# A graph layer with an edge index built beside its matrix products: pauses for the index, two conversions swapped in its round, and a split first load

## The chip, the cores and the metric

The kernel runs on one core of one Trainium2 chip. The metric is the device time of one execution in microseconds; a time with "median" is the median of several executions. The profile is of one execution, and its times count from the first instruction of the span.

## The reference

There are 1250 nodes with 1024 features, and 20000 edges, each with a source, a target and one of eight types. Cut to what matters, the reference computes:

```python
h = maximum(layernorm(x), 0)
u = h @ root + bias
for r in range(8):
    mask = (edge_type == r)
    sums = segment_sum(h[src] * mask[:, None], dst, 1250)
    cnt = segment_sum(mask, dst, 1250)
    u = u + (sums / maximum(cnt, 1)[:, None]) @ weight[r]
z = concatenate([u, h], 1) @ w_gate + b_gate
out = x + tanh(u) * z + h * (1 - z)
```

All tensors are float32. Since a mean times a matrix is the mean of the products, the kernel multiplies h by each weight first and gathers rows of the products.

## The kernel before, in words

**Products.** There are eleven 1024x1024 matrices: the eight weights, the root and the two halves of the gate. `step(s, i)` multiplies matrix `s` with a pair of 128-row blocks, `i` from 0 to 4, so a matrix takes five steps. A step is a 2x2 block scheme of Strassen's kind (`product`): up to seven groups of matmuls with 512 columns, each group shown in the trace as eight matmul records. From matrix 1 on, the steps with `i` below 4 leave out one group and put a second, smaller scheme in its place; its pieces of 256 columns (`Second`, L211, four records each) are `fill`s between the groups. After most groups ScalarE (ACT) copies the PSUM bank to an SBUF row: L313, L317, L321, L305 and L341 stand for the first, second, third, S3 and last group. The groups S4 and A12 are added by VectorE (DVE) instead, L298 and L331.

**Calls.** After each group, and after some fills, `product` calls `between(j)`. This makes 7 calls in a step and 35 in a matrix. `between` is `beside` in `step`. It issues the work of the next matrix: in the last step (`i` = 4) the differences of weight blocks `make_t1` (j=1), `make_t2` (j=4) and `make_t3` (j=5), in the first step of the next matrix `make_t4` (j=0) and, for matrices 1 to 3, one difference (`right`) in each of the calls 0 to 3 of the same step. All of these run on DVE (L166, L170, L174, L178, L201). After that `beside` calls `on(j)`.

**The index.** `on(j)` runs one more piece of the generator `index()`, up to its next `yield`. The index has 126 pieces: 18 of layer norm and columns, 86 of `slots`, and 22 of `order`. It begins in matrix 0. `slots` finds for every edge its place in the table of its target node. It takes 40 chunks of 512 edges; each round of its loop has two `yield`s, so it takes two calls:

- a call whose work is mostly ACT's (called the ACT call here): `as_bf16` (L796), four `one_hots` activations (L743) and their Relu (L745), `as_int` (L781, L783), `to_los` (L802, L803); also `load_keys`, which lets SP's queue load `k_bc` and `l_bc` (L774);
- the next call (called the PE call here): `count`, four small matmuls of TensorE (PE) on L761 and DVE additions on L766; `split` on DVE (L789); `place`, four small matmuls on L812, then DVE work (L817 to L836) and the scatters of GpSimd (POOL) on L840.

`place` reads what `to_los` and `as_bf16` made (`to_lo` and `s_b`), and `as_bf16` reads what `split` made. The PSUM tile `ps_n` of `count` has one buffer: the next `count` waits until L766 has read the last one.

`order` sorts nodes by number of edges (L894 on DVE) and lets POOL write and read the sorted tables (L506, L469). After matrix 3, `weights(0)` (L493 on DVE) reads those tables and the gathers of product rows begin (L1014 on POOL, L1022 on DVE).

**The order.** The order of instructions on each engine is the order in which the program issues them (`manual_schedule`); nothing is moved by a planner.

**The start.** `load_x` loads the first two blocks of x (`x0`) by SP's queue, one as two halves and one whole; then come the four blocks of the first matrix and more of x. The layer norm of both (`both`), their transposes (L257) and the copies (L259) stand ahead of the first product.

Of the kernel before, what the change touches and what calls it, by code (L numbers as in the profile page):

```python
# [19 lines left out]
def tile_rgcn_highway(  # L20
# [31 lines left out]
    nc = tc.nc  # L52
# [3 lines left out]
    P = 128  # L56
# [8 lines left out]
    NP = ND // 2  # L65
# [23 lines left out]
    def nrows(d):  # L89
        return min(P, N - d * P)  # L90
# [4 lines left out]
    def nedges(c):  # L95
        return P if c < NCH - 1 else EL
# [349 lines left out]
    steps = iter([(s, i) for s in range(NM - 1) for i in range(NP)])  # L446
# [78 lines left out]
    with ExitStack() as early:  # L525
# [6 lines left out]
        def load_x(i, part, t=None, pieces=1):  # L532
            d = i + part * NP
            n = nrows(d)
            if t is None:
                t = xpool.tile([P, D], F32, name="xt")
            for j in range(pieces):
                at = slice(j * D // pieces, (j + 1) * D // pieces)
                nc.sync.dma_start(t[:n, at], x[d * P:d * P + n, at])
            return t  # L540

        def scratch(i, part):
# [65 lines left out]


        warm = xpool.tile([P, 1], F32, name="warm")  # L610
        nc.scalar.activation(warm, eps, AF.Sqrt)
        x0 = [load_x(0, part, pieces=2 - part) for part in range(2)]
        fac[0].load_first()
        fac[0].load_next()
        fac[0].load_b22()
        x1 = [load_x(1, 0, scratch(NP - 2, 0))]
        fac[0].load_b21()
        x1.append(load_x(1, 1, scratch(NP - 2, 1)))
        x2 = [load_x(2, 0, h_op[2][:, S1:S2 + 1].rearrange("p a k f -> p (a k f)")), load_x(2, 1)]

# [7 lines left out]
        for name, of, pad in (("dst", dst, G * KEYS), ("typ", etype, R), ("src", src, 0)):  # L628
            t = ix0.tile([P, 2, P], I32, name=f"e_{name}")
# [97 lines left out]
        def slots(ix):  # L727
# [118 lines left out]
                    tc.add_to_no_dep_group("scatter", ins.ins)  # L846

            for j in range(ng + 3):
                for f, of in ((one_hots, j), (load_keys, j - 1), (as_int, j - 2), (to_los, j - 2),
                              (None, None), (count, j - 1), (split, j - 2), (place, j - 3),  # L850
                              (None, None), (as_bf16, j - 2)):
                    if f is None:
                        yield
                    elif 0 <= of < ng:
                        f(of)
# [115 lines left out]
        def index():  # L971
            for _ in zip_longest(norms(), columns()):
                yield
            with tc.tile_pool(name="ix", bufs=2) as ix:
                yield from slots(ix)
            yield from order()

        todo = index()
        going = [True]

        def on(j):
            if going[0]:
                going[0] = next(todo, 0) is None

        while going[0]:
            step(*next(steps), on)


    with ExitStack() as edges_part:
# [44 lines left out]
        def edges(g, blocks, to, late=0):  # L1034

            of = u_dram[g - 1] if g else None
            nb = len(blocks)  # L1040
            starts = [late + sum(K[g][d] for d in blocks[:b]) for b in range(nb + 1)]
            leaves = [starts[b + 1] - 1 + GOT for b in range(nb)]
            reads = [max(-1, starts[b] - 5, leaves[b - UB] if b >= UB else -1) for b in range(nb)]
            u, then = {}, {}
            for t in range(-1, leaves[-1] + 4):
                for b, d in enumerate(blocks):
                    if starts[b] <= t < starts[b + 1]:
                        k = t - starts[b]
                        add_slot(u[d], g, d, k, idx[:, g], w_of[:, g], first=g == 0 and k == 0)
                for b, d in enumerate(blocks):  # L1050
                    if t == leaves[b]:
                        then[t + 3] = to(d, u[d])
                if then.get(t):
                    then[t]()
                for b, d in enumerate(blocks):
                    if t == reads[b]:
                        u[d] = new_u(d, of, g)
                yield

        def u_back(g):  # L1060
            def to(d, u):
                n = nrows(d)
                to_rows(u_dram[g][:, :], u[:n], node[:n, g, d:d + 1], f"u{g}")

            return to
# [42 lines left out]
        def beside(e, total, s, i, last):  # L1108


            between = spread(e, total, 7 * ((last - s) * NP + NP - i))
            while s <= last:
                step(s, i, between)
                s, i = next(steps, (NM, 0))
            return s, i

        s, i = next(steps)
        while s <= R0[1]:
            step(s, i)
            s, i = next(steps)  # L1120
# [8 lines left out]
        def with_others(e):  # L1129

            others = other_groups()
            for k, _ in enumerate(e):
                yield
                if k % 2:
                    next(others, None)
            for _ in others:
                pass

        weights(0)
        s, i = beside(with_others(edges(0, range(ND), u_back(0))), sum(K[0]) + 2, s, i,  # L1140
                      R0[2] - 1)
# [6 lines left out]
        for g in range(1, G - 1):  # L1148
# [3 lines left out]
            s, i = beside(e, sum(K[g]) + LATE + 1, s, i, R0[g + 2] - 1)  # L1152
# [4 lines left out]
        with tc.If(passes > 0):  # L1157
# [30 lines left out]
            with tc.For_i(0, passes, 1):  # L1188
# [9 lines left out]
                for c in range(NCH):  # L1198
                    n = nedges(c)
# [92 lines left out]
        while s < NM - 1:  # L1292
# [8 lines left out]
            s, i = next(steps, (NM, 0))  # L1301

        for i in range(NP):
            t = [rows.tile([P, D], F32, name="row") for _ in range(2)]
# [59 lines left out]
```

## Time and profile before

| what | value |
|---|---|
| median of 3 executions | 1375.87 us (1373.83 to 1377.13) |
| the profiled execution: its own time | 1372.16 us |
| the profiled execution: span of the trace | 1370.3 us |
| mean granted TensorE clock | 0.997 |
| PE busy | 1349.8 us |
| DVE busy | 930.5 us |
| POOL busy | 638.7 us |
| ACT busy | 366.7 us |
| one later matrix, without the index (652.32 to 771.08 us) | 118.76 us |

The profiled execution's own time is its span and 1.9 us around it. It is 3.7 us shorter than the median of the three timed executions. A busy time counts the engine's own records; a wait is shown as the idle time ahead of an instruction, with the instruction that ended it. In the first 400 us the index lies beside the products, and ACT and DVE are busier than in the rest of the span.

### The profile page before, as it was taken

Reading aid. Unit: us, or ns where it says so; the run is one execution under the profiler, and the core shown is the slowest. Engines: PE = TensorE matmul, PEld = TensorE weight load, DVE = VectorE, ACT = ScalarE, POOL = GpSimd, SP = SyncE. Lnnn points to the kernel's source line nnn. Section 1 sums busy time; section 2 is a strip of 40 time slices with the busy share of each in tenths; the row PEclk is TensorE's granted clock in tenths of the full one; section 3 lists DMA queues with packets and bytes.
Section 4 is the critical chain, followed back from the end, with each engine's and each line's share of the span. In section 5 each row is a group of like instructions: output and inputs, shape, how many; then the busy total and the mean of one; then the engine's idle time right before and its main releaser. Section 6 shows DMA issues by size and latency. Waiting matters only on the chain.

```text
span 1370.3 us, 12737 instructions
## 1 busy us (share of the span) xinstructions
PE 1349.8 (99%) x3786; PEld 657.9 (48%) x3786; DVE 930.5 (68%) x1842; ACT 366.7 (27%) x793; POOL 638.7 (47%) x567
## 2 busy tenths in 40 slices
PE   7999999999999999999999999999999999999998
PEld 4444455445545544544554454455445445544443
DVE  6956987797678817556665746765564485567985
ACT  3336566566531111111111111111111111121220
POOL 0003655565561633647774334465443253436641
PEclk9999999999999999999999999999999999999999
DMA  8764665956553274379879627787955664586861
GB/s 306 286 204 103 125 139 142 182 108 130 141 132 104 65 216 121 115 235 252 233 268 323 210 103 269 278 291 253 356 202 207 225 243 142 189 293 222 288 204 58
DMA packets 110010, 272.77 MB, mean 199 GB/s; under 512 B 25906, under 2 KB 27936, under 8 KB 109808
## 3 DMA queue, kind: packets, MB, share of 16 engines
q0 software_dynamic: 48864, 128.60, 29.6%
q1 hardware_dynamic: 45232, 111.86, 27.0%
q10 hardware_dynamic: 15840, 31.46, 7.6%
q8 instruction: 30, 0.49, 0.1%
q14 instruction: 44, 0.36, 0.1%
HBM read 214.20 MB, written 80.65 MB: 215 GB/s over the span
## 4 chain that ended last, share of the span: by engine, by line
PE 79%; DVE 6%; issue 6%; DMA 2%; POOL 2%; ACT 1%; POOLq 0%; SPq 0%; DVEq 0%; ACTq 0%
PE ps L284 70%; PE ps L211 8%; DMA l_bc<-los_dram 1%; POOL got L469 1%; DVE seen L766 1%; DVE junk L826 1%; DMA got<-hr_dram,node 0%; DMA h_op<-z_dram,node 0%; PE ps_n L761 0%; POOL out_dram L475 0%; DVE row L1312 0%; DMA got<-y,idx 0%; DVE h_op L1258 0%; DVE u L1225 0%; DVE w L178 0%
## 5 line engine op out<-in xcount | busy, mean ns | idle before, releaser
L284 PE MATMUL ps<-w,h_op 128*128 128x512 f32 x2800 | 1226.8, 594 | 2.0 <-ACT row L321 2.0
L284 PEld LDWEIGHTS ps<-w,h_op 128*128 128x128 f32 x2800 | 527.6, 190 | 616.8 <-issue 600.6
L1014 POOL DMA_INDIRECT got<-y,idx x202 | 259.8, 1286 | 283.4 <-DVE u L1022 187.5
L1022 DVE SCALAR_TENSOR_TENSOR u<-got,w_of,u 128x1024 f32<-128x1024 f32 (+1 forms) x192 | 245.9, 1283 | 124.5 <-DMA got<-y,idx 122.3
L840 POOL DMA_INDIRECT table<-row_col,at_i x157 | 174.8, 1113 | 150.1 <-DVE at_i L836 75.2
L306 DVE TENSOR_TENSOR row<-row,part 128x512 f32<-128x512 f32 x55 | 38.0, 690 | 118.8 <-ACT part L305 118.8
L341 ACT COPY row<-ps 128x512 f32<-128x512 f32 x50 | 29.3, 586 | 236.2 <-PE ps L284 236.2
L298 DVE TENSOR_TENSOR row<-row,ps 128x512 f32<-128x512 f32 x55 | 37.7, 685 | 63.6 <-PE ps L284 56.2
L305 ACT COPY part<-ps 128x512 f32<-128x512 f32 x55 | 32.2, 586 | 177.3 <-PE ps L284 177.3
L313 ACT COPY row<-ps 128x512 f32<-128x512 f32 x55 | 32.2, 585 | 165.8 <-PE ps L284 159.2
L211 PE MATMUL ps<-w,w 128*128 128x256 f32 x288 | 71.3, 380 | 0.0
L321 ACT COPY row<-ps 128x512 f32<-128x512 f32 x55 | 32.2, 585 | 138.4 <-PE ps L284 138.4
L317 ACT COPY row<-ps 128x512 f32<-128x512 f32 x55 | 32.2, 585 | 135.5 <-PE ps L284 128.5
L211 PEld LDWEIGHTS ps<-w,w 128*128 128x128 f32 x288 | 54.4, 190 | 20.9 <-issue 15.3
L766 DVE TENSOR_TENSOR seen<-seen,ps_n 128x110 f32<-128x110 f32 x157 | 42.2, 269 | 27.6 <-PE ps_n L761 23.5
L826 DVE SCALAR_TENSOR_TENSOR junk<-k_bc,key_col,before 128x128 f32<-128x128 int32 x157 | 55.0, 350 | 4.2
L211 PE MATMUL ps<-w,h_op 128*128 128x256 f32 x216 | 55.9, 381 | 0.0
L506 POOL DMA_INDIRECT node_dram<-ids,pos_i x30 | 37.5, 1251 | 39.2 <-issue 39.2
L211 PEld LDWEIGHTS ps<-w,h_op 128*128 128x128 f32 x216 | 40.6, 190 | 25.8 <-issue 22.0
L743 ACT ACTIVATE is_lo<-io,less_lo 128x128 bf16<-128x128 f32 x157 | 50.4, 393 | 0.8 <-DVE row L306 0.8
L894 DVE SCALAR_TENSOR_TENSOR junk<-v_bc,val,one 128x1280 bf16<-128x1280 f32 x30 | 46.5, 1551 | 3.7 <-DMA v_bc<-val_dram 2.9
L469 POOL DMA_INDIRECT u<-u_dram,node x20 | 23.3, 1164 | 49.3 <-DMA last_dram<-u 32.8
(182 smaller groups left out, 953.2 us busy)
## 6 DMA issues: line engine op xcount, KB each, us to landing
y<-row SPq DMA_DIRECT2D x72, 512.0 KB, 5.5
w<-in_L_gnn_weight_dram ACTq DMA_DIRECT2D x21, 1024.0 KB, 7.2
w<-in_L_gnn_weight_dram SPq DMA_DIRECT2D x11, 1024.0 KB, 11.7
k_bc<-keys_dram SPq DMA_DIRECT2D x39, 256.0 KB, 4.0
l_bc<-los_dram SPq DMA_DIRECT2D x39, 256.0 KB, 6.9
w<-in_L_gnn_w_gate_dram ACTq DMA_DIRECT2D x6, 1024.0 KB
h_dram<-h_op SPq DMA_DIRECT2D x9, 512.0 KB, 6.8
hr_dram<-row SPq DMA_DIRECT2D x9, 512.0 KB, 4.0
```

What stands on the lines that cost most here:

```text
L211: nc.tensor.matmul(p, a[:, k, :], b[:, k, :], start=(fresh and k == 0), stop=(k == 1), skip_group_check=True)
L284: nc.tensor.matmul(b[:, at], aop[:, i, k, :], w.of[i][:, k, at], start=(fresh and k == 0), stop=(k == KQ - 1), skip_group_check=True)
L298: nc.vector.tensor_add(c12, c12, c)
L306: nc.vector.tensor_add(c22, c22, d)
L506: ins = nc.gpsimd.indirect_dma_start(out=node_dram[g][:, :], out_offset=bass.IndirectOffsetOnAxis(ap=pos_i[:, g, d:d + 1], axis=0), in_=id ...
L743: nc.scalar.activation(is_lo[:, i, :], io, AF.Abs, bias=less_lo[:, c0 + i:c0 + i + 1])
L766: nc.vector.tensor_add(seen[j][:, i, :], was, p[:, i, :])
L826: nc.vector.scalar_tensor_tensor(junk, o["k_bc"][:, i, :], key_col[:, c:c + 1], before, op0=OP.is_equal, op1=OP.mult, accum_out=rank[:, c: ...
L840: ins = nc.gpsimd.indirect_dma_start(out=table[:, :], out_offset=bass.IndirectOffsetOnAxis(ap=at_i[:n, i:i + 1], axis=0), in_=row_col[:n, ...
L894: nc.vector.scalar_tensor_tensor(junk, v_bc[:, g, :], val[:, c:c + 1], one.to_broadcast([P, KEYS]), op0=OP.is_gt, op1=OP.mult, accum_out=p ...
L1014: nc.gpsimd.indirect_dma_start(out=t[:n], out_offset=None, in_=y[g][:, :], in_offset=bass.IndirectOffsetOnAxis(ap=at[:n, d, k:k + 1], axis=0),
L1022: nc.vector.scalar_tensor_tensor(u[:n], t[:n], w, u[:n], op0=OP.mult, op1=OP.add)
```

## The change

Three edits:

1. In `load_x` the second half of a block that is loaded in pieces is issued by ACT's queue instead of SP's. Both blocks of `x0` are loaded in halves now, and these loads stand ahead of the activation that loads ACT's table.
2. In the loop of `slots`, `as_bf16` and `to_los` change places. `as_bf16` moves from the first to the last place of the ACT call; in the program's loop it is written for chunk j-3 of the new round instead of j-2 of the old one, which is the same call. `to_los` moves from the last place of the ACT call to the first place of the ACT call one round later.
3. `on(j)` runs no piece of the index in two calls of each matrix from matrix 1 on: step 0, call 0 and step 4, call 5. Later pieces of the index come that many calls later.

```diff
             for j in range(pieces):
                 at = slice(j * D // pieces, (j + 1) * D // pieces)
-                nc.sync.dma_start(t[:n, at], x[d * P:d * P + n, at])
+                (nc.scalar if j else nc.sync).dma_start(t[:n, at], x[d * P:d * P + n, at])
...
         warm = xpool.tile([P, 1], F32, name="warm")
+        x0 = [load_x(0, part, pieces=2) for part in range(2)]
         nc.scalar.activation(warm, eps, AF.Sqrt)
-        x0 = [load_x(0, part, pieces=2 - part) for part in range(2)]
...
             for j in range(ng + 3):
-                for f, of in ((one_hots, j), (load_keys, j - 1), (as_int, j - 2), (to_los, j - 2),
+                for f, of in ((one_hots, j), (load_keys, j - 1), (as_int, j - 2), (as_bf16, j - 3),
                               (None, None), (count, j - 1), (split, j - 2), (place, j - 3),
-                              (None, None), (as_bf16, j - 2)):
+                              (None, None), (to_los, j - 2)):
...
-        def on(j):
-            if going[0]:
-                going[0] = next(todo, 0) is None
-
         while going[0]:
-            step(*next(steps), on)
+            s, i = next(steps)
+
+            def on(j):
+
+                if s > 0 and (i, j) in ((0, 0), (NP - 1, 5)):
+                    return
+                if going[0]:
+                    going[0] = next(todo, 0) is None
+
+            step(s, i, on)
```

## The prediction

> **What bounds the kernel now.** I read the shares first, then who waited for whom on PE, then ACT's and PE's timelines where the index lies beside the products.
>
> ```profile
> PE 1349.8 (99%) x3786; PEld 657.9 (48%) x3786; DVE 930.5 (68%) x1842; ACT 366.7 (27%) x793; POOL 638.7 (47%) x567
> ```
>
> PE is busy 99% of the span. So a change can save only PE's idle time, 1370.3 - 1349.8 = 20.5 us with start and end, but it can add as much as it makes PE wait. PE's waits in the whole span (us in total, times, longest):
>
> ```profile
> PE ps L257 <- ACT h_op L575: 8.9, 3, 7.1
> PE ps_n L761 <- DVE seen L766: 2.7, 1, 2.7
> PE ps L284 <- ACT row L321: 2.0, 2, 1.9
> PE ps_q L812 <- ACT s_b L796: 0.6, 2, 0.4
> ```
>
> The first row is the start. The other three belong to the index. PE's timeline at the largest (start, length, then the instruction):
>
> ```profile
> 284.10 1.03 PE L211 MATMUL ps<-w,h_op 128*128 128x256 f32 x4
> 287.78 0.36 PE L761 MATMUL ps_n<-is_at,is_lo 128*128 128x110 bf16 x4 [2.65 <-DVE seen L766]
> 288.53 0.36 PE L812 MATMUL ps_q<-s_b,to_lo 128*128 128x60 bf16 x4 [0.39 <-ACT s_b L796]
> 288.70 8.48 PE L284 MATMUL ps<-w,h_op 128*128 128x512 f32 x16
> ```
>
> The sixteen records after the wait take 8.48 us where other sixteens take 7.11: the granted clock is 0.51 from 288 to 290 us and 0.63 from 290 to 292. The place is the change of matrix, where `make_t3`, `make_t4` (2.2 us each) and `right` crowd DVE.
>
> Now one ordinary round of the index, ACT from its copy L321 to its next copy:
>
> ```profile
> 130.76 0.59 ACT L321 COPY row<-ps 128x512 f32<-128x512 f32 x1 [2.50 <-PE ps L284]
> 131.24 0.40 ACT L796 CAST s_b<-s 128x240 bf16<-128x240 int32 x1
> 131.54 1.28 ACT L743 ACTIVATE is_lo<-io,less_lo 128x128 bf16<-128x128 f32 x4
> 132.85 0.63 ACT L745 ACTIVATE is_lo<-is_lo 128x512 bf16<-128x512 bf16 x1
> 133.39 0.20 ACT L781 CAST s_i<-seen 128x30 int32<-128x30 f32 x1
> 133.49 0.26 ACT L783 CAST s_i<-seen 128x90 int32<-128x90 f32 x1
> 133.99 0.72 ACT L802 ACTIVATE to_lo<-l_bc,less_pid 128x512 bf16<-128x512 int32 x1 [0.23 <-DMA l_bc<-los_dram]
> 134.75 0.63 ACT L803 ACTIVATE to_lo<-to_lo 128x512 bf16<-128x512 bf16 x1
> 138.02 0.59 ACT L305 COPY part<-ps 128x512 f32<-128x512 f32 x1 [2.65 <-PE ps L284]
> ```
>
> and PE in the same time:
>
> ```profile
> 127.05 7.11 PE L284 MATMUL ps<-w,h_op 128*128 128x512 f32 x16
> 133.99 0.36 PE L761 MATMUL ps_n<-is_at,is_lo 128*128 128x110 bf16 x4
> 134.20 0.27 PE L812 MATMUL ps_q<-s_b,to_lo 128*128 128x60 bf16 x4
> ```
>
> ACT waits for PE's group (2.50 us), copies, does the ACT call, and waits again (2.65 us): ACT is never ahead of PE. One group later, at 134.20, PE's `place` reads `s_b`. Before, `s_b` is the first thing of the ACT call: done at 131.64, 2.56 us early.
>
> **What the Trainium skill says.** "PSUM — Partial Sum Buffer", section "Engine vs sequencer instructions": the queues of ScalarE and VectorE are strict FIFO, and matmuls start in program order. The trace agrees: L796 waited for `split` 28.0 us in 15 times and everything behind it on ACT waited too. "TensorE: Matmul & The Clock Gate", section "What's actually happening": an idle window of about 3.4 us halves the clock. Here about 3.4 us of nearly idle PE (285.1 to 288.5) brought 0.51, and the 1.85 us wait at 157.2 brought no drop. "DMA: Bandwidth & Descriptors", section "Issuing engines are not separate DMA queues": issuing from two engines saves only the sequencer's issue time. The trace shows that price: SP's three issues of x took 1.35 us, 0.45 each.
>
> **The change part by part.**
>
> *Pauses (edit 3).* They move the pieces out of the calls with `make_t3` and `make_t4`. Together with edit 2 they should end the waits in the middle of the span: 1.85 (157.2; L321 stood behind an ACT call that waited for `split`), 2.65, 0.39 and 0.21 (280 to 288.5), 0.15 (367.5), in sum 5.25, and 8.48 - 7.11 = 1.37 of slow clock: **-6.6 us**. Least is about -3, if DVE stays late. The price: two pauses in matrix 1, two in 2, one in 3, so the index ends 5 calls later, 5 x 118.76/35 = 17 us. Its cover: the last read of `idx` leaves POOL at 480.2 and DVE reads it at 521.8; POOL then waits from 494.9 to 531.5. 17 fits into 36, so nothing is paid; were the cover gone, it would be up to 17 us. SP's loads of `k_bc`, `l_bc` and `v_bc` and POOL's scatters keep their places to these pieces, and the stores of y that they pass on SP wait for nothing of theirs: nothing.
>
> *The swap (edit 2).* It issues the same instructions. `to_los` a round later gives `l_bc` about 7 us more to land, which ends ACT's 13.2 us of waits for it; on PE that is in the sum above. But `s_b` becomes the last thing of the ACT call. With the starts of the rows shown, and 0.54 and 0.17 from L803 and L783 to a next instruction that does not wait (150.05 to 150.59, 149.13 to 149.30): 0.76 + 0.54 (`to_los`) + 1.31 + 0.54 (`one_hots`) + 0.10 + 0.17 (`as_int`) + 0.40 (L796) = 3.82 us. From 131.24 that is 135.06, and 0.05 until PE sees it (280.42 to 280.47): 135.11, where PE wants it at 134.20. **Each such round makes PE wait 0.91 us.** Behind the waiting `place` stands the next group of the product, so the wait is on the path. On DVE, L817 waits for it too, with `seen` and `split` already done.
>
> The size depends on what PE has between the group whose copy stands before the ACT call and the `place`. I followed all ACT calls in the new order of instructions, calls written (matrix: step,call):
> - One full group (3.43 us): 0: (4,0) (4,2) (4,4); 1: (0,4) (0,6) (2,0) (3,1) (4,0) (4,2); 2: (0,1) (1,6) (2,1) (3,0) (3,4) (3,6). 15 x 0.91 = 13.7 us.
> - Only one fill of four records (0.86 us): 1: (0,2); 2: (2,5) (3,2). 0.91 + 3.43 - 0.86 = 3.48; 3 x 3.48 = 10.4 us.
> - A fill of eight (1.73 us): 1: (1,1). 2.6 us.
> - One group and a small fill (0 to 0.05 us each), and the short last chunk (0.5): 0.6 us.
> - Two groups, or an ACT call after a group that DVE evicts, where ACT starts a group earlier: nothing.
>
> Sum **+27.3 us**. Bounds: if DVE's lateness delays L781, up to 0.3 more each (+5); if I misplace the copy by 0.3 us, -6. The three waits of 3.48 lie at the length that cost 1.37 us of clock; that is 0 to 4.1, and I take half, **+2.1**.
>
> *The first loads (edit 1).*
>
> ```profile
> 3.44 0.69 DVE L558 BATCH_NORM_STATS2 st<-xt 128x6 f32<-128x512 f32 x1 [3.44 <-DMA xt<-in_x_dram]
> 4.43 0.69 DVE L558 BATCH_NORM_STATS2 st<-xt 128x6 f32<-128x512 f32 x1 [0.30 <-DMA xt<-in_x_dram]
> 7.46 1.29 DVE L558 BATCH_NORM_STATS2 st<-xt 128x6 f32<-128x512 f32 x2 [1.37 <-DMA xt<-in_x_dram]
> ```
>
> The second block holds DVE 1.37 us, and PE's first product waits for both blocks. Issues in parallel bring it up to 0.9 us earlier (two issues), and at most 1.37. The bytes are the same on the same 16 engines, and two halves in flight can delay the first one: +0.4 at worst. SP's weights are issued 0.45 us earlier. ACT's two issues push its table load (0.74, 1.28 us long) to about 1.6; ACT's next work is at 5.40, so this costs nothing. I take **-0.5 us** (-1.2 to +0.4).
>
> Sum: -6.6 + 27.3 + 2.1 - 0.5 = +22.3 us on the profiled execution's 1372.16: 1394.5. The median is 3.7 above that execution, so **1398 us**.
>
> **The rivals.**
> - *Faster.* `s_b` is in time because ACT runs its calls ahead of PE; then only the savings count: 1375.9 - 7.1 = 1369. It decides from the point where ACT begins its call 0.91 us before the copy ends. For it: ACT is busy only 27%. Against it: the 2.50 and 2.65 us that ACT waits for PE around the shown call, with a FIFO queue. 10%.
> - *Heavier.* All four long waits halve the clock and DVE delays L781: 1398 + 2 + 5, to 1409. 14%.
> - *Half.* Part of the rounds escape (about half of the 0.91s and one long wait): 1398 - 10 = 1388, down to 1383. 12%.
> - *Does not do what it says.* A conversion "a round later" could relax its reader, but `as_bf16` stays in the same call; only `to_los` is a round later. If `place` moved too, savings and nothing more: inside the first rival.
> - *Nothing.* Long waits and savings cancel within 0.2%: 4%.
>
> **How the numbers follow.** The main case has 60% and its own range 1391 to 1404. With most of the heavier and half cases the range is 1386 to 1408. 0.2%, 2.75 us, is about what a measurement of this kernel can tell from no change. Slower 60 + 14 + 12 = 86%, same 4%, faster 10%.
>
> **What would show it.** In the profile after: "PE ps_q L812 <- ACT s_b L796" grows from 0.6 us to 20 to 30 us in about 20 waits, the longest near 3.5; the other two PE waits on the index and ACT's on `l_bc` are gone; POOL's first gather at about the same distance from matrix 4; first product 0.5 us earlier. If that L812 wait stays under 5 us, I am wrong.

## The result, and the profile after

The changed kernel takes **1397.66 us** (median of 6 runs, 1395.11 to 1400.6) against 1375.3 us for the kernel before (6 runs on the same chip, 1372.66 to 1377.13). The ratio is 1.0165 [1.0149, 1.0181], so it is slower by 22.4 us. The profiled execution of the changed kernel took 1398.4 us with a span of 1396.6 us; that is 26.3 us more span than the profile before.

The shares on the page of the kernel after, engine by engine:

```profile
PE 1357.5 (97%) x3786; PEld 661.1 (47%) x3786; DVE 931.6 (67%) x1842; ACT 364.5 (26%) x793; POOL 636.4 (46%) x567
```

The number of instructions shown is the same for every engine as before. PE's idle time, 1396.6 - 1357.5, grew from 20.5 to 39.1 us, and its busy time grew by 7.7 us for the same 3786 records. The first is waits; most of the second is a lower clock, as the next views show. PE's waits after (us in total, times, longest):

```profile
PE ps_q L812 <- ACT s_b L796: 17.9, 12, 3.3
PE ps L257 <- ACT h_op L575: 8.0, 2, 7.5
PE ps_q L812 <- ACT s_i L781: 3.1, 3, 1.7
PE ps_q L812 <- ACT s_i L783: 2.9, 4, 0.7
PE ps_q L812 <- issue: 0.7, 1, 0.7
```

Four of the five rows are one and the same wait, `place` for ACT. The profile put some of the 20 cases down to another instruction of the same ACT call or to none, but the idle time of an ordinary round is the same 0.72 us whichever is named. Together they are 24.6 us. The rows that stood here before, `ps_n` for DVE and `ps` for the copy L321, are gone.

ACT's timeline of the kernel after, one ordinary round, from its copy L321 to its next copy:

```profile
130.04 0.59 ACT L321 COPY row<-ps 128x512 f32<-128x512 f32 x1 [3.40 <-PE ps L284]
130.52 0.72 ACT L802 ACTIVATE to_lo<-l_bc,less_pid 128x512 bf16<-128x512 int32 x1
131.28 0.63 ACT L803 ACTIVATE to_lo<-to_lo 128x512 bf16<-128x512 bf16 x1
131.81 1.26 ACT L743 ACTIVATE is_lo<-io,less_lo 128x128 bf16<-128x128 f32 x4
133.11 0.63 ACT L745 ACTIVATE is_lo<-is_lo 128x512 bf16<-128x512 bf16 x1
...
133.64 0.20 ACT L781 CAST s_i<-seen 128x30 int32<-128x30 f32 x1
133.75 0.26 ACT L783 CAST s_i<-seen 128x90 int32<-128x90 f32 x1
133.92 0.39 ACT L796 CAST s_b<-s 128x240 bf16<-128x240 int32 x1
138.18 0.59 ACT L305 COPY part<-ps 128x512 f32<-128x512 f32 x1 [3.88 <-PE ps L284]
```

Nothing in this call waits: ACT works straight through from 130.52 to 134.31 (133.92 + 0.39), 3.79 us, and `s_b` is its last product. PE in the same time, in the same kernel:

```profile
133.27 0.36 PE L761 MATMUL ps_n<-is_at,is_lo 128*128 128x110 bf16 x4
134.35 0.27 PE L812 MATMUL ps_q<-s_b,to_lo 128*128 128x60 bf16 x4 [0.72 <-ACT s_b L796]
134.47 7.11 PE L284 MATMUL ps<-w,h_op 128*128 128x512 f32 x16
141.41 0.37 PE L761 MATMUL ps_n<-is_at,is_lo 128*128 128x110 bf16 x4
142.50 0.28 PE L812 MATMUL ps_q<-s_b,to_lo 128*128 128x60 bf16 x4 [0.72 <-ACT s_b L796]
```

From `count` to `place` it is 1.08 us now (133.27 to 134.35), where it was 0.21 (133.99 to 134.20). So a round costs 0.88 us (from the unrounded starts), of which the row shows 0.72; the rest lies under the end of `count`, which the profile models. The whole round is 8.14 us (141.41 - 133.27). The next product group stands behind `place`, so all of it is on the path.

The places with only a fill between ACT's copy and `place`, in PE's timeline of the kernel after:

```profile
161.34 0.28 PE L812 MATMUL ps_q<-s_b,to_lo 128*128 128x60 bf16 x4 [3.29 <-ACT s_b L796]
161.45 8.81 PE L284 MATMUL ps<-w,h_op 128*128 128x512 f32 x16
...
189.19 0.32 PE L812 MATMUL ps_q<-s_b,to_lo 128*128 128x60 bf16 x4 [2.42 <-ACT s_b L796]
...
388.14 0.36 PE L812 MATMUL ps_q<-s_b,to_lo 128*128 128x60 bf16 x4 [3.29 <-ACT s_b L796]
388.32 9.97 PE L284 MATMUL ps<-w,h_op 128*128 128x512 f32 x16
```

The fourth is at 370.19, also 3.29 us. Read the line after each wait too: sixteen records of L284 take 8.81 and 9.97 us instead of 7.11. Windows of the kernel after show why (span of the window, length, busy time of PE, PEld, DVE, ACT and POOL with their instructions, then the granted clock, DMA share and GB/s):

```profile
162.00:164.00 2.00, 2.00 (x4) 0.95 (x3) 1.82 (x11) 0.00 (x0) 1.03 (x2) 0.50 0.48 83
190.00:192.00 2.00, 2.00 (x3) 0.67 (x2) 1.86 (x10) 0.00 (x0) 0.00 (x0) 0.50 0.00 0
371.00:373.00 2.00, 2.00 (x3) 0.67 (x2) 1.83 (x10) 0.00 (x0) 0.42 (x1) 0.50 0.03 5
389.00:391.00 2.00, 2.00 (x3) 0.67 (x2) 1.86 (x10) 0.00 (x0) 0.00 (x0) 0.50 0.01 0
```

PE looks fully busy in these windows, but on half a clock. What the granted clock lacks to 1.00, added up over all windows of 1 us from 20 to 460 us, is 1.7 us in the profile before and 8.5 us after.

Last, the start of the kernel after, from the timelines of DVE, PE and ACT:

```profile
4.26 1.29 DVE L558 BATCH_NORM_STATS2 st<-xt 128x6 f32<-128x512 f32 x2 [4.26 <-DMA xt<-in_x_dram]
...
6.43 1.28 DVE L558 BATCH_NORM_STATS2 st<-xt 128x6 f32<-128x512 f32 x2
7.50 4.03 PE L257 MATMUL ps<-ident,h_op 128*128 128x128 f32 x16 [7.50 <-ACT h_op L575]
11.33 4.91 PE L284 MATMUL ps<-w,h_op 128*128 128x512 f32 x10
15.20 0.59 ACT L313 COPY row<-ps 128x512 f32<-128x512 f32 x1 [3.89 <-PE ps L284]
```

and of the kernel before, PE and ACT in the same stretch:

```profile
12.37 4.04 PE L284 MATMUL ps<-w,h_op 128*128 128x512 f32 x6
17.31 0.59 ACT L313 COPY row<-ps 128x512 f32<-128x512 f32 x1 [4.96 <-PE ps L284]
```

The first block comes 0.8 us later than before (3.44), the second is used 1.0 earlier (7.46, and no wait now). The transposes run without a gap, and the first product starts at 11.33 instead of 12.37. ACT's first copy of a product (L313) starts at 15.20 instead of 17.31: one half of these 2.1 us is the earlier start, the other a faster first group (3.9 us from its start to the copy instead of 4.9). Before, six records took 4.04 us; after, ten took 4.91. Both profiles give the granted clock as 1.00 in all of the first 20 us, so they don't show what made the records before slower.

Where the span went, by the first copy L313 of each matrix:

| from the first copy of | before | after | difference |
|---|---|---|---|
| start to matrix 0 | 17.31 | 15.20 | -2.1 |
| matrix 0 to 1 | 133.28 | 135.30 | +2.0 |
| matrix 1 to 2 | 126.08 | 140.42 | +14.3 |
| matrix 2 to 3 | 130.44 | 141.51 | +11.1 |
| matrix 3 to 4 | 118.80 | 119.78 | +1.0 |
| each later matrix | 118.76 | 118.76 | 0 |

The sum is +26.3 us, all of it where the index runs.

### The profile page after: what moved, and what is told of

It reads as the page before. It is cut to its first block, busy times and chain, and to the rows that moved or that the text cites. A ratio compares the mean times of both kernels' runs of the same rounds, so it can differ in the third digit from the quotient of the medians.

```text
span 1396.6 us, 12766 instructions
## 1 busy us (share of the span) xinstructions
PE 1357.5 (97%) x3786; PEld 661.1 (47%) x3786; DVE 931.6 (67%) x1842; ACT 364.5 (26%) x793; POOL 636.4 (46%) x567
## 4 chain that ended last, share of the span: by engine, by line
PE 78%; issue 6%; ACT 5%; DVE 3%; POOL 1%; DMA 1%; SPq 0%; POOLq 0%; ACTq 0%; DVEq 0%
PE ps L284 69%; PE ps L211 7%; ACT is_lo L743 2%; ACT to_lo L802 1%; ACT to_lo L803 1%; POOL got L469 1%; PE ps_q L812 1%; DMA got<-hr_dram,node 1%; ACT is_lo L745 0%; POOL out_dram L475 0%; DVE row L1317 0%; DMA got<-y,idx 0%; DVE h_op L1263 0%; DVE row L1318 0%; DMA y<-row 0%
## 5 line engine op out<-in xcount | busy, mean ns | idle before, releaser
L284 PE MATMUL ps<-w,h_op 128*128 128x512 f32 x2800 | 1232.1, 596 | 0.0
L284 PEld LDWEIGHTS ps<-w,h_op 128*128 128x128 f32 x2800 | 529.9, 191 | 617.7 <-issue 602.9
L1019 POOL DMA_INDIRECT got<-y,idx x202 | 256.3, 1269 | 272.9 <-DVE u L1027 204.3
L840 POOL DMA_INDIRECT table<-row_col,at_i x157 | 180.3, 1148 | 184.2 <-DVE at_i L836 106.5
L313 ACT COPY row<-ps 128x512 f32<-128x512 f32 x55 | 32.2, 585 | 177.3 <-PE ps L284 166.7
L321 ACT COPY row<-ps 128x512 f32<-128x512 f32 x55 | 32.2, 586 | 151.6 <-PE ps L284 151.6
```

The source lines that it names most:

```text
L284: nc.tensor.matmul(b[:, at], aop[:, i, k, :], w.of[i][:, k, at], start=(fresh and k == 0), stop=(k == KQ - 1), skip_group_check=True)
L840: ins = nc.gpsimd.indirect_dma_start(out=table[:, :], out_offset=bass.IndirectOffsetOnAxis(ap=at_i[:n, i:i + 1], axis=0), in_=row_col[:n, ...
L1019: nc.gpsimd.indirect_dma_start(out=t[:n], out_offset=None, in_=y[g][:, :], in_offset=bass.IndirectOffsetOnAxis(ap=at[:n, d, k:k + 1], axis=0),
```

## The experiments

The theory was the prediction's: `s_b` comes last out of a FIFO call that starts only when PE's group has ended, and PE waits for it in each of some 20 rounds. The rivals were that the pauses or the split load carry the loss, and that the work on ACT, not its order, does it. Each kernel is compared with the kernel before on the same chip.

### Each edit alone, and the two without the swap

The swap alone (`e1_swap` is the kernel before with this):

```diff
-    (as_int, j - 2), (to_los, j - 2), (None, None), ..., (None, None), (as_bf16, j - 2)
+    (as_int, j - 2), (as_bf16, j - 3), (None, None), ..., (None, None), (to_los, j - 2)
```

> Edit 2 alone (as_bf16 last in the ACT call, to_los a round later), no pauses, old loads. Theory (place on PE waits for s_b, now the last thing of the ACT call): with no pauses the calls fall otherwise, but the count is nearly the same: 16 rounds with one full group of cover x 0.91, three with a fill of four x 3.48, one with a fill of eight x 2.6, in sum 27.6 us, with PE's waits on L812 about 25 us in the profile; with 3 to 6 us of slow clock and some of the old 6.6 us gone, the time is 22 to 32 us above the kernel before. Rival (the pauses, or the index that ends later, are the cost): within 5 us of the kernel before. Rival (the late to_los is the cost): slower too, but PE then waits for ACT to_lo, L803, and not for L796.

It took 1397.79 us against 1373.36, ratio 1.0168 [1.0145, 1.019]. PE's waits on `place`, and what is left of the wait for DVE, in the profile of this kernel:

```profile
PE ps_q L812 <- ACT s_b L796: 20.4, 16, 3.3
...
PE ps_n L761 <- DVE seen L766: 0.3, 1, 0.3
```

So the swap by itself makes the whole loss. The second row was not expected to be so small: the wait for DVE at the change of matrix shrinks from 2.7 to 0.3 us without any pause. A PE that is late at every round may simply find DVE ready; `e8_later_no_pauses` below fits that, since there PE is in time, and the wait is back.

The pauses alone (`e2_pauses`):

```diff
+    if s > 0 and (i, j) in ((0, 0), (NP - 1, 5)):
+        return
```

> Edit 3 alone (no piece of the index in calls 0,0 and 4,5 from matrix 1 on). Theory: the three waits on the index in the middle of the span (1.85, 3.3 with its slow clock, 0.15) go and nothing comes in their place: 4 to 7 us faster than the kernel before, no wait of PE above 0.5 us after the start. Rival (pauses push the index past its cover): slower than before, POOL's first gather or DVE's L493 late and PE waiting near matrix 4. Rival (DVE's crowding at the change of matrix stays): 0 to 2 us faster.

1367.18 us against 1373.36, ratio 0.9954 [0.9939, 0.997]. All waits of PE in its profile:

```profile
PE ps L257 <- ACT h_op L575: 9.2, 3, 7.2
PE ps L284 <- ACT row L321: 1.0, 1, 1.0
```

The pauses end the wait for DVE and cost nothing that shows. One wait of 1.0 us stayed where none above 0.5 was expected. It is behind ACT's copy L321, as the 1.85 us before were, and ACT still waits for `split` in this kernel: 15.4 us in 11 times, where it was 28.0 us in 15.

The split load alone (`e3_load`, and the same kernel once more on another chip as `e9_load_again`):

```diff
-    nc.sync.dma_start(t[:n, at], x[d * P:d * P + n, at])
+    (nc.scalar if j else nc.sync).dma_start(t[:n, at], x[d * P:d * P + n, at])
...
+    x0 = [load_x(0, part, pieces=2) for part in range(2)]
     nc.scalar.activation(warm, eps, AF.Sqrt)
-    x0 = [load_x(0, part, pieces=2 - part) for part in range(2)]
```

> Edit 1 alone (second halves of the first x by ACT's queue). After the whole change the first copy of the first product came 2.1 us earlier (15.20 against 17.31). Theory: that is this edit's, and PE keeps it to the end: 1.5 to 2.5 us faster than the kernel before. Rival (DVE, 80 to 90% busy up to 60 us, takes it back): 0 to 0.7 us faster, with a longer wait of PE on ACT h_op L575 between 40 and 90 us.

1373.53 us against 1373.36, ratio 1.0007 [0.9996, 1.0017]: no gain, though its first copy L313 stood at 15.44, 1.9 us ahead of before. The expected 1.5 us or more did not come. Its profile shows a new wait of 1.51 us that has no named cause, on PE and ACT:

```profile
185.50 0.59 ACT L321 COPY row<-ps 128x512 f32<-128x512 f32 x1 [1.76 <-PE ps L211]
186.14 3.70 PE L284 MATMUL ps<-w,h_op 128*128 128x512 f32 x8 [1.51 <-issue]
```

PE goes on 0.05 us after ACT's copy L321 ends. Why that copy starts only at 185.50 is not shown. A second profile (`e9_load_again`) tells whether this wait belongs to the kernel:

> Edit 1 alone once more, for a second profile. In the first one, PE's first product came 1.9 us earlier and PE then waited 1.5 us at 186 us with no releaser named, at a place where the kernel before did not wait. Theory (the gain is given back at that place whenever the index runs without pauses): that wait is there again, 1.0 to 1.7 us, and the time is within 1 us of the kernel before. Rival (that wait was an event of one execution): it is gone, and the time is 1 to 2.5 us below the kernel before.

1371.41 us against 1372.3, ratio 0.9996 [0.9988, 1.0005]. The wait at 186 is not there. Neither expectation came in full: the wait is gone, but the time did not fall by 1 us or more. The first copy stood at 14.70, and part of the loss is elsewhere, PE's timeline of this kernel:

```profile
157.16 5.40 PE L284 MATMUL ps<-w,h_op 128*128 128x512 f32 x8 [1.84 <-ACT row L321]
```

The wait itself is the one of before (1.85), but here eight records took 5.40 us, at half the clock, where a group of eight in the same profile took 3.60 (at 185.47). In both profiles the lead is given back while the index runs. At the first copy of matrix 1 they are still 1.6 and 1.9 us ahead of before, at that of matrix 3 0.6 and 0.5 us behind. At which places it is lost differs between the two, and why is not settled.

The load and the pauses together, without the swap (`e4_load_pauses`, the changed kernel with the diff of the swap undone):

```diff
-    (as_int, j - 2), (as_bf16, j - 3), (None, None), ..., (None, None), (to_los, j - 2)
+    (as_int, j - 2), (to_los, j - 2), (None, None), ..., (None, None), (as_bf16, j - 2)
```

> Edits 1 and 3 without the swap. Theory: all of the savings and none of the cost: 6 to 9 us faster than the kernel before, PE's waits on L812 under 1 us. Rival (the pauses or the loads carry the cost): slower than before.

1365.88 us, ratio 0.9945 [0.993, 0.9959]. It is 1.3 us ahead of the pauses alone on the same chip. So with most waits of the middle out of the way (two of 1.1 and 0.7 us are left in its profile), a good part of the load's lead stays. The same two edits that stand in a kernel 22 us slower make it 7.5 us faster once the swap is undone.

### The order in the call, or the work in it

`e5_bf16_second` keeps everything of the change, `to_los` a round later too, and moves only the conversion up again, right behind `to_los`:

```diff
-    (as_int, j - 2), (as_bf16, j - 3), (None, None), ..., (None, None), (to_los, j - 2)
+    (as_int, j - 2), (None, None), ..., (None, None), (to_los, j - 2), (as_bf16, j - 2)
```

> The kernel after with as_bf16 (chunk j-2) right behind to_los (chunk j-2) at the head of the ACT call; to_los stays a round later, loads and pauses stay. Theory (the place of as_bf16 in the ACT call sets the wait): s_b is ready 0.76 + 0.54 + 0.40 = 1.70 us into the call instead of 3.82, that is 2.12 us earlier: the rounds with one full group wait for nothing, the three with a fill of four about 1.4 us each, the one with a fill of eight about 0.5; 24 to 31 us faster than the kernel after, 2 to 7 us faster than the kernel before. Rival (the late to_los is the cost): to_lo is as late as in the kernel after, the time stays within 6 us of it.

1368.48 us against 1373.63, ratio 0.9963 [0.9949, 0.9976], and 29.2 us below the change's median. (The change was timed beside a kernel before of 1375.3, so 1.7 us of the 29.2 may be the setting.) PE's wait in its profile:

```profile
PE ps_q L812 <- ACT s_b L796: 4.4, 5, 1.2
```

It is three waits of 1.17 us at the places with one fill, and two of 0.31 and 0.58. The same instructions, with one of them 2.1 us earlier in the call (behind L803 instead of behind L783, 131.81 against 133.92 in the round shown), decide between loss and gain. `to_lo` is as late here as in the change, so the late `to_los` is not the cost.

`e6_extra` goes the other way: the change, with one more activation of 128x512 ahead of the conversion, whose output nothing reads.

```diff
-    (as_bf16, j - 3),
+    (extra, j - 3), (as_bf16, j - 3),
...
+    def extra(j):
+        spare = ix.tile([P, CG, P], BF16, name="spare", bufs=1)
+        nc.scalar.activation(spare, io[:, None, :].to_broadcast([P, CG, P]), AF.Relu, scale=-1.0, bias=1.0)
```

> The kernel after with one more activation (128x512, into a spare tile that nothing reads) just ahead of as_bf16. Theory: s_b comes 0.54 to 0.76 us later in each of 40 rounds, and each of the 19 rounds that wait waits that much longer, the five that are just in time 0.5 more each: 12 to 18 us slower than the kernel after. Rival (the time lost does not hang on the length of the ACT call): within 3 us of the kernel after, as ACT is busy 26%.

1407.07 us against 1373.63, ratio 1.025 [1.0231, 1.0268]. That is 9.4 us above the change by the medians, 11 by what each adds to its own kernel before, and below the range expected. PE's wait in its profile, and one ordinary round (`place` has line 817 in this kernel):

```profile
PE ps_q L817 <- ACT s_b L796: 34.8, 23, 3.8
...
135.08 0.28 PE L817 MATMUL ps_q<-s_b,to_lo 128*128 128x60 bf16 x4 [1.24 <-ACT s_b L796]
```

Each ordinary wait grew by 0.52 us, from 0.72 to 1.24, and the extra activation takes 0.53 us from its start to the next instruction's (125.46 to 125.99). The long waits grew by the same, 3.29 to 3.81. So in these rounds the time put ahead of `s_b` in the call is paid in full, which is what a FIFO (instructions in strict order) on the path does. The waits grew by 10.2 us in all, which is by itself less than the 12 expected at the least: the extra activation took 0.53 us and not up to 0.76, the rounds that were just in time gave little, and the wait of 1.70 us became one of 1.24. The clock's share shrank too: what it lacked was 5.1 us here and 8.5 in the change. Behind one of the three waits of 3.81 us the clock stayed full:

```profile
163.00:165.00 2.00, 1.90 (x8) 0.96 (x8) 1.48 (x7) 0.05 (x1) 1.21 (x2) 1.00 0.22 43
```

So the whole is less than expected on both counts.

### The reader moved along

If the wait is `place` asking in the same round, a `place` one round later must end it. `e7_place_later` is the change with

```diff
-    is_at = ix.tile([P, CG, NHI + NTB], BF16, name="is_at", bufs=4)
+    is_at = ix.tile([P, CG, NHI + NTB], BF16, name="is_at", bufs=5)
...
-    t = now[j][name] = ix.tile([P, CG, P], I32, name=name, bufs=3)
+    t = now[j][name] = ix.tile([P, CG, P], I32, name=name, bufs=4 if name == "k_bc" else 3)
...
-    for j in range(ng + 3):
+    for j in range(ng + 4):
...
-    (count, j - 1), (split, j - 2), (place, j - 3)
+    (count, j - 1), (split, j - 2), (place, j - 4)
```

> The kernel after with place, too, one round later (chunk j-4; k_bc 4 and is_at 5 buffers, one more round of the loop). Theory: the conversion gets the round that the change's words promise it, s_b is ready about 6 us before place wants it: no wait on L812, 5 to 9 us faster than the kernel before. Rival (something else in the change costs): more than 5 us slower than the kernel before.

**1363.42 us** (1363.17 to 1363.55), ratio 0.9927 [0.9913, 0.9941]: 10.2 us faster than the kernel before, a little more than the 5 to 9 expected, and the lowest median of all kernels here. Whether it beats the load and the pauses without the swap (`e4_load_pauses`, 0.9945 [0.993, 0.9959] on another chip) the times don't show, since the intervals overlap; its profile has neither of the two waits that are left there. In PE's row of waits only the start is left, and PE's timeline has a round again without a gap (`place` is L813):

```profile
PE ps L257 <- ACT h_op L575: 7.7, 2, 7.2
...
131.97 0.36 PE L761 MATMUL ps_n<-is_at,is_lo 128*128 128x110 bf16 x4
132.18 0.28 PE L813 MATMUL ps_q<-s_b,to_lo 128*128 128x60 bf16 x4
132.29 7.11 PE L284 MATMUL ps<-w,h_op 128*128 128x512 f32 x16
139.24 0.37 PE L761 MATMUL ps_n<-is_at,is_lo 128*128 128x110 bf16 x4
```

0.21 us from `count` to `place`, and 7.27 from round to round. ACT's call is the same as in the change, `s_b` still its last product; only nobody waits for it. The granted clock was 1.00 all through the index.

`e8_later_no_pauses` is this kernel without the pauses:

```diff
-    if s > 0 and (i, j) in ((0, 0), (NP - 1, 5)):
-        return
```

> The kernel with place a round later (k_bc 4 and is_at 5 buffers) and with the loads, but without the pauses. Theory: with s_b in time, DVE's crowding at the change of matrix shows again, since only the pauses relieve it: PE waits for DVE seen L766 near 285 us about 2 to 3 us, with slow clock behind it; 3 to 6 us slower than the same kernel with pauses (1363.4), so 1366 to 1370. Rival (the late conversion alone removes the old waits, by letting ACT not wait for split, and the pauses are worth nothing): 1363 to 1365.

1368.07 us against 1372.3, ratio 0.9971 [0.9961, 0.9981]: 4.7 us more than with them by the medians, 6 us by the two ratios. PE's timeline has the old wait for DVE again, and what follows it:

```profile
283.51 0.36 PE L761 MATMUL ps_n<-is_at,is_lo 128*128 128x110 bf16 x4 [2.01 <-DVE seen L766]
...
284.28 8.81 PE L284 MATMUL ps<-w,h_op 128*128 128x512 f32 x16
```

2.0 us of wait and 1.7 us of clock (8.81 - 7.11): the pauses relieve the crowding at the change of matrix, and with PE in time nothing else does. The wait behind L321 is not there, though, in this kernel without pauses: ACT waits for `split` only 0.9 us.

## Why the prediction was right, and where it was not

**Right: the price of the swap, place by place.** The prediction said that ACT is never ahead of PE, that the call takes 3.82 us up to `s_b`, and that a round loses 0.91 us. Measured: 3.79 us, and 0.88 us. Of the fifteen places with one group between, fourteen show the wait of 0.71 or 0.72 us, and the fifteenth (268.24) 1.70: ACT's copy there begins 2.25 us ahead of `count` (263.93 to 266.18) instead of 3.23 (130.04 to 133.27). The three places with one small fill cost 3.45 each (predicted 3.48), the one with a fill of eight 2.6 (2.6), the short last chunk 0.6 (0.6 with the small fills). The sum is 14 x 0.88 + 1.9 + 3 x 3.45 + 2.6 + 0.6 = 27.8 us, where the prediction had 27.3. `e5_bf16_second` and `e6_extra` show that it is the place in the call that is paid for, and `e7_place_later` that it is paid only because `place` asks in the same round.

**Right: the waits removed, -6.6, and each edit has its own.** The old waits are gone, with the slow clock behind one of them. The prediction gave the credit to the pauses and the swap together and did not divide it. The profiles do. The swap ends ACT's waits for `split` (28.0 us before, 0.4 in the change) and for `l_bc` (13.2 and 0.4), and with them PE's wait behind L321: none in `e1_swap` or `e8_later_no_pauses`, 1.0 us with the pauses alone. The pauses end the wait for DVE: none in `e2_pauses`, 2.0 us in `e8_later_no_pauses`; the 0.3 us of `e1_swap` come with a late PE. In a kernel where PE is late each hides part of the other's work. The times of the single edits (+24.4, -6.2 and +0.2, sum 18.4) and of the whole (+22.4) agree with an overlap of that kind, but their intervals are too wide to show it.

**Right: the pauses' price, nothing.** POOL in the timeline of the kernel before:

```profile
531.49 1.95 POOL L1014 DMA_INDIRECT got<-y,idx  x1 [36.62 <-DVE u L1020]
```

DVE and POOL in that of the kernel after:

```profile
548.86 0.36 DVE L493 SCALAR_TENSOR_TENSOR w_of<-idx 128x200 f32<-128x200 int32 x1
...
558.53 1.95 POOL L1019 DMA_INDIRECT got<-y,idx  x1 [23.75 <-DVE u L1025]
```

POOL still waits 23.75 us for DVE there, where it was 36.6. So the later end of the index took 13 us of the cover, less than the 17 us reckoned, and none of it reached the path.

**Mis-sized: the slow clock.** The step "0 to 4.1, and I take half, +2.1" gave 8.5 us. It failed in two ways. It let only the three waits of 3.48 count, yet the one of 2.42 us halved the clock as well. And it priced a drop at 1.37 us from one group, where the sum over the windows says 1.7 for the same place; after the wait at 388.14 the clock stayed at 0.50 for about twice as long and cost 3.4. The rival "heavier" had this half right: all four long waits did halve the clock, but DVE did not delay L781 by 0.3 in every round.

**Mis-sized: the first loads.** -0.5 was taken, with -1.2 as the lower end; the first product started 1.0 us earlier and its first copy 2.1. The step counted the issue time only. The Trainium skill, "DMA: Bandwidth & Descriptors", section "Issuing engines are not separate DMA queues", says that a second engine saves just that, 0.45 us an issue in this trace. The trace has 1.0 us on the second block and 0.8 us lost on the first (0.4 was the worst reckoned), so more than the issue time changed; the second block also comes in two halves now, and no run here separates these. The step also had no term for the first group, which ran 1.0 us faster. How much of the 2.1 us reaches the end is another matter: nothing measurable alone, 1.3 us beside the pauses.

**Mis-sized: from the profile to the median.** +3.7 us was added since the median before stood that far above its profiled execution. After, the profiled execution stands 0.7 us above the median. So the change in the profiles is +26.2 and in the medians +22.4. The terms of the sum, 27.8 + 8.5 - 6.6 - 2.1 = 27.6, come within 1.4 us of the profiled +26.2, or 1.1 if the old slow clock is taken at 1.7 us as well; that rest is not placed. The forecast of the sum was +22.3, short by 4, and the offset was too high by about as much. The mechanism and its largest term were right, but that the number came within 1 us of the median is partly two errors that cancel.

## What to carry to other kernels

When work is given to a FIFO engine beside a product, ask of each result not only in which round it is made but in which place of its call, and what stands between that call's start and the reader: here 2.6 us of earliness was spent and 22 us lost without an instruction added. If a producer is moved back, move its reader back by a round as well and pay with buffers, as `e7_place_later` does. And price a PE wait of about 2 us or more at more than its length: in these profiles nearly every such wait cost 1.7 us of clock besides.

## What the hardware showed that was not expected

- **The clock after an idle PE.** In seven profiles (before, after and five of the experiments) there are 16 waits of PE of 1.98 us or more beside the index, and 15 were followed by a granted clock of 0.50, which then lasted about 3.4 us and cost 1.7 us each (once 3.4). The exception is the wait of 3.81 us shown above. Of three waits of 1.83 to 1.85 us one was followed by it; of those of 1.70 us and less, none. The Trainium skill, "TensorE: Matmul & The Clock Gate", section "What's actually happening", puts the idle window near 3.4 us and says that it runs freely, so that the same kernel can meet it at another phase. The length of the drop agrees, about 3.4 us; the trigger does not, since 2.0 us of waiting, with a few small matmuls around it, was enough here. A free phase would suit the mixed outcome at 1.84 us, but no run here shows the phase.
- **The spread between runs.** The kernels whose profile shows no slow clock in the index (`e2_pauses`, `e4_load_pauses`, `e5_bf16_second`, `e7_place_later`) spread by 1.9, 0.4, 0.9 and 0.4 us between runs; the change and `e1_swap` by 5.5 and 7.3. The mean clock granted to each run is on record and accounts for part of this. Of the nine runs of `e8_later_no_pauses`, the three at 0.999 took 1366.7 to 1366.9 us and the six at 0.997 or 0.998 took 1367.9 to 1368.4. It is not the whole: beside `e1_swap` the 19 runs of the kernel before, all at 0.997 or 0.998, took 1370.5 to 1376.7 us. What else differs between them is open.
